# A graph layer whose rows are fetched one by one: three groups more of lead, and one place more in the ring

## The chip, the cores and the metric

The kernel runs on one core of a Trainium2 chip. Its time is the device time of one execution in microseconds. Beside it stands a profile: one further execution, recorded by the hardware profiler.

The engines are named as the profile names them: PE is TensorE (PEld its weight loads), DVE is VectorE, ACT is ScalarE, POOL is GpSimd and SP is SyncE. SP, ACT and POOL also issue DMAs, each from a queue of its own, and each engine works through its own instructions in order.

## The reference

x has 12500 rows (nodes) of 256 numbers. There are 200000 edges; edge e leads from node src[e] to node dst[e], and the edges are sorted by dst. All is float32.

```python
h = jnp.maximum(_layernorm(x, axis=-1), 0.0)
agg = jax.ops.segment_sum(h[src], dst, num_segments=N)
z = (1.0 + eps_gin) * h + agg
t = jnp.dot(z, W1) + b1                          # 256 -> 512
t = jax.nn.relu(_batchnorm(t, g1, bt1))          # over all 12500 rows
conv_out = jnp.dot(t, W2) + b2                   # 512 -> 256
out = x + jax.nn.relu(_batchnorm(conv_out + h, g2, bt2))
```

So for each edge a row of h is gathered, rows with the same destination are summed, and two dense layers follow, each with a normalisation that needs sums over all nodes.

## The kernel before, in words

**Groups.** The 200000 edges are cut into tiles of 128 edges and the tiles into 131 groups of 12 (GT); the last group has 3. Since the edges are sorted, the 1536 edges of a group lead to few neighbouring nodes. The loop over groups (L789 to L847, and a second one from L856 for the last five) is written out by hand: the order in which each engine gets its instructions is the order in the source.

**One group, i.** POOL gathers its rows, 128 at a time, with one indirect DMA for each tile (`gather`, L567). DVE builds a matrix of zeros and ones from the destinations (`edges`, L606). PE multiplies the two and adds up over the 12 tiles (`sums`, L625, the matmul on L639). The sums are copied (`hold`), brought to their place by a second matmul (`put`, L696) and added by DVE into a chunk zc of 512 nodes (`add`, L707). Chunks are loaded by SP from a table h_cols (`z_load`, L597) and scaled by ACT (`z_scale`). A chunk whose groups are all in is multiplied by W1 (`slice_of`, L719), its statistics are taken, and the product is stored by ACT in a table t_tab (`take`, L735).

**Lead-in.** The rows of h must be computed first. While that is done (NCH is 25 chunks of 512 rows), the first 30 groups (LEAD) gather rows of x and normalise them after the gather. From group 30 on POOL gathers rows of h from the table h_tab.

**Where gathered groups lie.** `gather(i + AHEAD)` is issued at step i, with AHEAD 3. In the lead-in the groups go round four places (L569): some are tiles of the pool `ring`, with RING buffers, the others the pairs `lands` (gta with 8 tiles, gtb with 4), which the first two groups used too. From group 33 on (L570) all groups go to `ring` alone. POOL may write into a place when PE has summed the group that lay there.

**Rows fetched one by one.** To take work from POOL, two queues each fetch one tile out of every nine groups: `hf` on SP (tile 0 of the group, called one_s) and `af` on ACT (tile 1, one_a). A `Fetcher` (L454) begins at step 28; at each step it issues the next lot of single-row DMAs (L500), 128 rows in nine steps (SP_PACE and ACT_PACE are (9, 1)), in lots of 16 (LOADS), after loading their addresses into registers (L494). Which groups it serves is settled on L463: `begin + SPARE + 9 * k`, for k = 1, 2, and so on. The set for such a group is asked for in the nine steps that end SPARE + 1 steps before it. Before PE uses a fetched tile it waits for a semaphore that counts the 128 rows (`use`, L508); within a group these tiles come last (L632). SP also issues the loads of zc, and ACT the stores of t_tab, in the same queues and in program order.

**After the loop** the second half of the kernel (from L905) loads t_tab, applies the first normalisation, multiplies by W2, and so on. Its tiles lie where the loop's tiles lay.

Of the kernel before, what the change touches and what calls it, by code (L numbers as in the profile page):

```python
# [22 lines left out]
LEAD = 30  # L23
EARLY = 2
FRONT = 3
RING = 2
LOW = 8
LOADS = 16
SP_PACE = (9, 1)
ACT_PACE = (9, 1)  # L30
SPARE = 4
XIN = 1


# [7 lines left out]
def kernel(  # L42
# [306 lines left out]
    def fast():  # L349
# [24 lines left out]
        with ExitStack() as fs:  # L374
# [14 lines left out]
            with ExitStack() as es:  # L389
                ln = es.enter_context(tc.tile_pool(name="ln", bufs=2))  # L390
                ring = es.enter_context(tc.tile_pool(name="ring", bufs=RING))
                sel = es.enter_context(tc.tile_pool(name="sel", bufs=2))
# [61 lines left out]
                class Fetcher:  # L454

                    def __init__(self, eng, kind, table, pace, begin, end, slots, tag):
# [5 lines left out]
                        while True:  # L462
                            g = begin + SPARE + -(-(len(self.groups) + 1) * self.over // self.per)  # L463
                            if g >= end:
# [102 lines left out]
                def gather(i):  # L567
                    t0, n = groups[i]
                    k = i % (AHEAD + 1)  # L569
                    if i >= LEAD + AHEAD or k > AHEAD - RING:  # L570
                        ga = ((0, GT, ring.tile([P, GT, D], F32, name="gt")),)
# [880 lines left out]
```

## Time and profile before

| what | value |
|---|---|
| median of 3 runs | 2481.28 us (2460.36 to 2487.5) |
| the profiled execution | 2484.16 us |
| its span, first to last instruction | 2482.4 us |
| mean granted TensorE clock | 0.766 of full speed |
| busy, PE / PEld / DVE / ACT / POOL | 62% / 40% / 34% / 17% / 62% |
| gathers from h_tab, POOL (L578) | 1171, 948 ns each in the middle |
| rows fetched one by one, SP and ACT (L500) | 1280 each |

"Idle before" a group of instructions is time in which its engine had nothing running, and the name behind the arrow is what ended that time: an engine and line, a DMA, "issue" (the engine waited for nothing that the profile shows) or "remote" (a semaphore whose sender the profile doesn't name). A name with a small q (SPq, ACTq) is the engine's queue, where DMAs are issued. In a timeline a line is: start, length, engine, source line, operation, tiles written and read, count, and in brackets the idle time before it. A line with a count over 1 merges several instructions. Matmuls in float32 have two records for each tile, so a group shows 24.

### The profile page before, as it was taken

What the parts mean: (1) busy time and instruction counts of PE and PEld (TensorE: products, weight loads), DVE (VectorE), ACT (ScalarE), POOL (GpSimd) and SP (SyncE); (2) the same over time, 40 slices, a digit from 0 to 9 for tenths busy, and PEclk for the clock granted to TensorE, in tenths of its full rate; (3) what the DMA queues carried; (4) which work ended last, traced back from release to release, by engine and by line L of the source; (5) the groups of instructions that cost most, each with busy time, mean ns of one, the idle gap of its engine ahead of it and who ended that gap; (6) DMA issues with size and microseconds to landing.
All of it is one profiled execution on the core that took longest, in us unless ns stands there. A gap on an engine that the chain in (4) does not pass through costs nothing.

```text
span 2482.4 us, 20597 instructions
## 1 busy us (share of the span) xinstructions
PE 1530.5 (62%) x4856; PEld 1003.3 (40%) x4856; DVE 852.0 (34%) x1344; ACT 424.8 (17%) x777; POOL 1540.6 (62%) x1589
## 2 busy tenths in 40 slices
PE   2564566555766665666655565656556666656997
PEld 1453444434434443434433344334333443434445
DVE  5454455432222222222222122122211222222897
ACT  4465455530000000000000000000000000001554
POOL 7566666565566666676666666665666666653550
PEclk9676777777777776777777777777777776777999
DMA  6566666443343333333433333343334333542988
GB/s 175 164 207 200 190 191 195 146 121 95 104 119 101 112 110 110 108 108 108 118 100 113 104 112 112 109 114 101 108 107 118 107 106 108 159 140 74 320 310 338
DMA packets 150290, 349.84 MB, mean 141 GB/s; under 512 B 32956, under 2 KB 63308, under 8 KB 150158
## 3 DMA queue, kind: packets, MB, share of 16 engines
q0 software_dynamic: 74048, 202.28, 29.2%
q1 hardware_dynamic: 45688, 105.80, 12.3%
q10 hardware_dynamic: 30422, 40.35, 4.7%
q8 instruction: 41, 0.67, 0.1%
q14 instruction: 91, 0.75, 0.1%
HBM read 284.29 MB, written 64.00 MB: 140 GB/s over the span
## 4 chain that ended last, share of the span: by engine, by line
issue 27%; POOL 20%; PE 16%; another core or an unknown queue 14%; SPq 11%; DVE 6%; ACT 4%; DMA 2%; PEld 0%; ACTq 0%; DVEq 0%; PEldq 0%; POOLq 0%
POOL gt L578 20%; SPq L500 10%; PE ps L639 6%; PE one L991 2%; PE ph L727 2%; DVE stg L422 2%; PE pq L991 1%; PE pr L991 1%; PE pz L702 1%; ACT gta L446 1%; DMA gt<-h_tab,srcT 1%; DVE oh L610 1%; SPq L494 1%; ACT ht L446 1%
## 5 line engine op out<-in xcount | busy, mean ns | idle before, releaser
L578 POOL DMA_INDIRECT gt<-h_tab,srcT x1171 | 1110.2, 948 | 601.7 <-issue 343.5
L639 PE MATMUL ps<-gt,oh 128*128 128x256 f32 x2648 | 841.3, 449 | 427.4 <-issue 286.7
L639 PEld LDWEIGHTS ps<-gt,oh 128*128 128x128 f32 x2648 | 559.2, 221 | 690.2 <-issue 373.4
L604 ACT ACTIVATE zc<-zc,gin 128x1024 f32<-128x1024 f32 (+1 forms) x25 | 28.1, 1125 | 1594.1 <-issue 979.3
L702 PE MATMUL pz<-at,zs 128*128 128x256 f32 x516 | 186.2, 474 | 156.3 <-issue 149.6
L689 DVE COPY zs<-ps 128x256 f32<-128x256 f32 x97 | 40.7, 420 | 649.0 <-remote 407.5
L738 DVE BATCH_NORM_STATS2 st<-ph 128x6 f32<-128x512 f32 x96 | 66.4, 693 | 495.8 <-remote 452.8
L727 PE MATMUL ph<-zc,w1s 128*128 128x512 f32 (+1 forms) x392 | 201.7, 640 | 40.9 <-DVE hc L561 25.9
L610 DVE TENSOR_TENSOR oh<-col,dstT 128x1536 f32<-128x1536 f32 x129 | 225.1, 1746 | 0.0
L578 POOL DMA_INDIRECT gt<-in_x_dram,srcT x168 | 159.3, 948 | 88.7 <-issue 57.1
L702 PEld LDWEIGHTS pz<-at,zs 128*128 128x128 f32 x516 | 123.1, 241 | 218.7 <-issue 200.0
L717 DVE TENSOR_TENSOR zc<-pz,zc 128x512 f32<-128x512 f32 (+7 forms) x185 | 91.7, 519 | 213.4 <-remote 127.4
L578 POOL DMA_INDIRECT gta<-in_x_dram,srcT x112 | 106.2, 948 | 50.6 <-issue 25.1
L727 PEld LDWEIGHTS ph<-zc,w1s 128*128 128x128 f32 x392 | 83.1, 214 | 107.0 <-issue 63.6
L549 PE MATMUL ph<-ident,ht 128*128 128x128 f32 x196 | 41.9, 346 | 108.1 <-issue 58.9
L639 PE MATMUL ps<-gta,oh 128*128 128x256 f32 x272 | 71.5, 398 | 39.9 <-issue 39.7
L446 ACT ACTIVATE gt<-gt,nbg,rsg 128x256 f32<-128x256 f32 x168 | 85.0, 588 | 11.9 <-issue 10.1
L549 PEld LDWEIGHTS ph<-ident,ht 128*128 128x128 f32 x196 | 29.3, 175 | 126.1 <-issue 77.3
L578 POOL DMA_INDIRECT gtb<-in_x_dram,srcT x56 | 53.1, 948 | 39.8 <-issue 11.6
L639 PE MATMUL ps<-gtb,oh 128*128 128x256 f32 x136 | 51.4, 524 | 42.7 <-issue 22.8
L639 PEld LDWEIGHTS ps<-gta,oh 128*128 128x128 f32 x272 | 54.3, 200 | 52.3 <-issue 45.5
L639 PE MATMUL ps<-one_s,oh 128*128 128x256 f32 x20 | 9.1, 546 | 104.0 <-DMA one_s<-h_tab 57.0
(195 smaller groups left out, 1308.7 us busy)
## 6 DMA issues: line engine op xcount, KB each, us to landing
t_tab<-ts ACTq DMA_DIRECT2D x96, 256.0 KB
one_s<-h_tab SPq DMA_DIRECT2D x1280, 1.0 KB
one_a<-h_tab ACTq DMA_DIRECT2D x1280, 1.0 KB
gt<-h_tab,srcT POOLq DMA_INDIRECT x1171
xt<-in_x_dram SPq DMA_DIRECT2D x24, 512.0 KB
h_tab<-ht ACTq DMA_DIRECT2D x24, 512.0 KB
h_cols<-hc SPq DMA_DIRECT2D x24, 512.0 KB
zc<-h_cols SPq DMA_DIRECT2D x24, 512.0 KB
```

Of the source, the lines that this page charges most:

```text
L422: nc.vector.bn_stats(st[:, c : c + 2, :].rearrange("p c s -> p (c s)"), two.rearrange("p c d -> p d c"),)
L446: nc.scalar.activation(slot(to, c), slot(v, c), AF.Relu, bias=nb[:, c : c + 1], scale=rs[:, c : c + 1])
L500: d = self.eng.dma_start(self.tiles[g][q % P : q % P + 1, q // P, :].bitcast(U8), self.bytes[bass.ds(v, 4 * D)].rearrange("(o e) -> o e", ...
L549: nc.tensor.transpose(ph[:, c * P : (c + 1) * P], ht[:, c, d * P : (d + 1) * P], ident)
L578: nc.gpsimd.indirect_dma_start(out=slot(ga, t - t0)[:rows], out_offset=None, in_=x if i < LEAD else h_tab, in_offset=bass.IndirectOffsetOn ...
L610: nc.vector.tensor_tensor(ohs[i][:, :n, :], col[:, :P].unsqueeze(1).to_broadcast([P, n, P]), dstT[:, t0 : t0 + n].unsqueeze(2).to_broadcas ...
L639: nc.tensor.matmul(ps, lhsT=oh[:rows, j, :], rhs=fetched[:rows], start=(j == order[0]), stop=(j == order[-1]))
L702: nc.tensor.matmul(pz[:, d, :n], lhsT=zs[:, d * P : (d + 1) * P], rhs=at[:, :n], start=True, stop=True)
L717: nc.vector.tensor_add(side, pz[:, :, a - lo : b - lo], side)
L727: nc.tensor.matmul(ph[:, :n], lhsT=w1s[:, d, f * P : (f + 1) * P], rhs=zc[c][:, d, :n], start=(d == 0), stop=(d == DC - 1),)
L738: nc.vector.bn_stats(st1[:, f, c, :], ph[:, :n])
L991: nc.tensor.matmul(ps, lhsT=w[:, k, :], rhs=t[:, k, :], start=(k == 0), stop=(k == DC - 1))
```

## The change

Two constants. SPARE sets how many groups ahead of its use a fetched set has to be complete (L463); with 7 in place of 4 the groups that use fetched tiles are 44, 53, ... 125 and no more 41, 50, ... 122. They are ten for each queue, as before. RING is the number of buffers of the pool that holds gathered groups; in the lead-in (L570) three of the four places are then tiles of the ring and one is a pair of `lands`, and from group 33 on three groups can lie gathered, not two. A buffer takes 12 KB of each partition.

```diff
 EARLY = 2
 FRONT = 3
-RING = 2
+RING = 3
 LOW = 8
 LOADS = 16
 SP_PACE = (9, 1)
 ACT_PACE = (9, 1)
-SPARE = 4
+SPARE = 7
 XIN = 1
```

## The prediction

> **What bounds the kernel now.** I read the views in this order: the page, the stretches by stage, POOL's own order of time, the waits of the fetched rows, and SP's queue. The profiled execution took 2484.16 us, of which the span is 2482.4; the runs shown have a median of 2481.28, so the sum below starts at 2484.2 and stands 3 us above that median. A measurement of this kernel can tell about 1% (25 us) from no change: its three runs lie 27 us apart.
>
> The page's head, and the stretches, each with its length and the busy time of PE, PEld, DVE, ACT, POOL:
>
> ```profile
> span 2482.4 us, 20597 instructions
> ...
> 40.00:532.50 492.50, 274.58 (x1002) 205.27 (x1003) 241.80 (x446) 263.21 (x551) 313.53 (x332) 0.73 0.57 177
> 532.50:892.50 360.00, 227.05 (x704) 149.70 (x704) 94.46 (x143) 20.89 (x38) 230.18 (x243) 0.76 0.37 107
> 892.50:1199.60 307.10, 190.38 (x562) 121.27 (x561) 72.67 (x108) 3.44 (x3) 202.38 (x215) 0.73 0.38 110
> 1199.60:2118.80 919.20, 550.01 (x1673) 358.66 (x1672) 216.46 (x322) 11.48 (x10) 599.35 (x633) 0.74 0.38 109
> 2118.80:2284.00 165.20, 97.88 (x316) 65.52 (x316) 32.97 (x58) 8.84 (x16) 89.63 (x95) 0.76 0.44 132
> 2284.00:2482.40 198.40, 183.04 (x572) 96.98 (x572) 170.58 (x222) 106.83 (x142) 75.95 (x34) 0.97 0.84 305
> ```
>
> The first is the lead-in, the last the second half of the kernel, which the change leaves as it is. Between them, POOL is the pace: 215 gathers in 307.1 us are 1.428 us each, 633 in 919.2 us are 1.452. What one takes without a wait, and what comes on top, is in POOL's timeline (start, length, idle before and its releaser):
>
> ```profile
> 987.50 0.95 POOL L578 DMA_INDIRECT gt<-h_tab,srcT  x1 [4.67 <-remote]
> ...
> 1016.35 0.95 POOL L578 DMA_INDIRECT gt<-h_tab,srcT  x1 [0.30 <-issue]
> 1022.01 0.95 POOL L578 DMA_INDIRECT gt<-h_tab,srcT  x1 [4.71 <-remote]
> 1023.26 0.95 POOL L578 DMA_INDIRECT gt<-h_tab,srcT  x1 [0.31 <-issue]
> ...
> 1053.75 0.95 POOL L578 DMA_INDIRECT gt<-h_tab,srcT  x1 [4.49 <-remote]
> ```
>
> A gather is followed by the next 1.25 us later. Every 34.5 us (987.50 to 1022.01: two groups, 24 gathers) POOL stops for 4.5 to 4.7 us. That looks like a ring with too few places; what PE and DVE do just before the stop says more:
>
> ```profile
> 999.62 1.88 PE L727 MATMUL ph<-zc,w1s 128*128 128x512 f32 x4
> ...
> 1010.18 0.59 PE L639 MATMUL ps<-gt,oh 128*128 128x256 f32 x1 [2.21 <-issue]
> 1012.98 0.59 PE L639 MATMUL ps<-gt,oh 128*128 128x256 f32 x1 [2.22 <-issue]
> ...
> 1021.60 0.70 DVE L738 BATCH_NORM_STATS2 st<-ph 128x6 f32<-128x512 f32 x1 [17.23 <-remote]
> ...
> 1023.24 6.67 PE L639 MATMUL ps<-gt,oh 128*128 128x256 f32 x24
> 1029.75 1.03 PE L702 MATMUL pz<-at,zs 128*128 128x256 f32 x4
> ```
>
> While POOL gathers, PE falls to one matmul in 2.8 us, with "issue" as the reason, that is for nothing the profile shows. About 4 us after POOL has stopped it is fast again (24 matmuls in 6.67 us), and only then do DVE and POOL see what PE had finished long before: DVE's statistics at 1021.60 had waited 17.23 us for a slice that PE had done at 1001.5. SP is in the same state: its register move takes 29 ns in the middle and up to 1420.
>
> ```profile
> L500 SPq MOVE one_s<-h_tab x1280: 1/29/1420, 499.7 to 2149.6; - x183
> L500 SPq DMA_DIRECT2D one_s<-h_tab x1280: 2/228/1422, 500.1 to 2151.0; - x183
> ```
>
> So the stop is not only a wait for a place; it is also when PE, SP and ACT get their work through. Two groups per stop is the pace, and a third place does not change what PE gets done per stop. I give this reading more weight than any other, though its cause cannot be seen.
>
> **The change part by part.** *SPARE 4 to 7.* The ten fetched sets of rows per queue stay ten; the groups that use them move from 41, 50, ... 122 to 44, 53, ... 125. SP and ACT issue the same instructions in the same order, no DMA more or less; POOL leaves out the same 20 gathers, three groups later. What it aims at are PE's waits for one_s:
>
> ```profile
> 754.35 0.59 PE L639 MATMUL ps<-one_s,oh 128*128 128x256 f32 x2
> ...
> 1060.23 0.59 PE L639 MATMUL ps<-one_s,oh 128*128 128x256 f32 x2
> ...
> 1533.36 1.22 PE L639 MATMUL ps<-one_s,oh 128*128 128x256 f32 x2 [20.81 <-PEq L510]
> 1693.19 1.22 PE L639 MATMUL ps<-one_s,oh 128*128 128x256 f32 x2 [27.92 <-DMA one_s<-h_tab]
> 1845.79 1.22 PE L639 MATMUL ps<-one_s,oh 128*128 128x256 f32 x2 [16.82 <-DMA one_s<-h_tab]
> 2002.79 1.22 PE L639 MATMUL ps<-one_s,oh 128*128 128x256 f32 x2 [26.18 <-PEq L510]
> 2150.42 1.22 PE L639 MATMUL ps<-one_s,oh 128*128 128x256 f32 x2 [12.23 <-DMA one_s<-h_tab]
> ```
>
> Five waits, 104 us of PE. But PE is not the pace. Four of them lie in the stretch to 2118.8, and there a gather took 1.452 us against 1.428 in the stretch without waits: 0.024 x 633 = 15 us is the most that the four can have cost. Per group the two stretches give 17.06 us (307.1 / 18, groups 50 to 68) and 17.02 (919.2 / 54, to group 122): by that count they cost nothing. The bounds are 0 and 15, and up to 12 more for the fifth.
>
> How many waits go? SP issued 1280 rows from 500.1 to 2151.0: 1.29 us each, 165 us for a set, against 153.5 us for nine groups at 17.06. It loses 11.5 us per set, and over nine sets 104. The first set was there at about 500 + 165 = 665, 89 us before its use at 754; three groups more make that 140, which lasts for all ten. But SP owes part of its rate to the waits, in which POOL stops too. Here is a stretch without any:
>
> ```profile
> 1171.61 42.27 SPq L500 DMA_DIRECT2D one_s<-h_tab  x27
> ```
>
> That is 1.57 us a row, 201 for a set; at this rate SP falls 47 us behind per set and is late again from the fourth or fifth on. So I expect two or three short waits to stay, late in the loop, and take 8 us of the 0 to 27 as gained.
>
> *RING 2 to 3.* Behind the lead-in POOL then needs the sums of a group one earlier. In the steady part I cost this at nothing, by the reading above. Its effect is at the two ends. Where the rotation of four places ends, and in the last groups, POOL waits for PE by name:
>
> ```profile
> 629.97 0.95 POOL L578 DMA_INDIRECT gt<-h_tab,srcT  x1 [12.74 <-PE ps L639]
> ...
> 2167.14 0.95 POOL L578 DMA_INDIRECT gt<-h_tab,srcT  x1 [4.92 <-remote]
> 2228.89 0.95 POOL L578 DMA_INDIRECT gt<-h_tab,srcT  x1 [16.97 <-PE ps L639]
> ```
>
> The first should shrink to an ordinary stop of 4.7 (8 us gained), the second should go (17 gained), since the place that it waits for is then that of the group before. Against it, PE has one group more to sum when POOL is done: undisturbed 6.67 us, with the placing (1.03) and a slice (1.88) 9.6.  Net about 16; the bounds are 0 (PE's late groups set the end anyway) and 25.
>
> In the lead-in four places rotate as before, but only one of them, not two, is the split pair of tiles gta and gtb, which can be refilled piece by piece. POOL's waits at gta, of what the two pairs show the larger part, are
>
> ```profile
> POOL gta L578 <- remote: 16.1, 8, 4.6
> ```
>
> 2 us each; seven groups with a whole tile instead lose between 0 and 16 us, and I take 4.
>
> The tiles of the second half keep their addresses, and the third place lies under yT tiles. SP loads those when the last sum (the first line) is over, so nothing is later there:
>
> ```profile
> L681 PE MATMUL pz<-oh,gt x12: 272/275/340, 2282.3 to 2283.7; 128*128 128x84 f32 x8, 64*128 64x84 f32 x4
> ...
> 2295.49 2.49 SPq L974 DMA_DIRECT2D yT<-h_cols  x4
> ```
>
> The sum: 2484.2 - 8 - 16 + 4 = 2464.
>
> **The rivals.** *Slower, by long bursts.* The point that decides is whether PE's news of the group before the last reaches POOL before it has done 24 gathers. If it does, POOL goes on to 36 while PE stands at one matmul in 2.8 us, and the stop after it is longer. The trace has one burst of 36, from 2167.1 to 2211.9, with the stop of 16.97 behind it:
>
> ```profile
> 2167.10:2228.90 61.80, 34.13 (x37) 0.78 0.49 153
> ```
>
> 61.8 us for 36 gathers are 1.717 each. For all 1171 gathers of the loop that would be 1171 x (1.717 - 1.44) = 324 us, 2808 (1.44 is 34.5 / 24); with a stop of 8 us, 36 x 1.253 + 8 = 53.1, 1.475 each, 41 us, 2525. I take the near end, since nothing but the loop's end shows the long stop. Against it: in the steady part what PE finished 14 us after a stop (the slice at 1001.5, POOL having started again at 987.5) wasn't seen before the next, and with three places PE, a group further behind, finishes the deciding group after 1.7 groups of 9.6 us, at about 16.
>
> *Nothing moves.* SP stays the bound for the late groups, so rows asked for 7 groups ahead are no more complete 7 ahead than now 4; and if the row waits go, the loads of zc, which stand in SP's queue behind the rows, are late in their place. They nearly are now:
>
> ```profile
> 1824.05 0.36 SPq L600 DMA_DIRECT2D zc<-h_cols  x1
> ...
> 1827.86 1.15 ACT L604 ACTIVATE zc<-zc,gin 128x1024 f32<-128x1024 f32 x1 [103.71 <-DMA zc<-h_cols]
> ...
> 1829.04 0.29 DVE L717 TENSOR_TENSOR zc<-pz,zc 128x128 f32<-128x128 f32 x1 [4.55 <-issue]
> ```
>
> DVE adds into that chunk 5 us after its load was issued. PE may run about two and a half groups further before the adds hold it, no three. Then only the ends gain, and the lead-in's loss eats that: 2480.
>
> *The ring is simply short.* Then a third place removes the stops: 1171 x (1.43 - 1.255) = 205 us, 2279. SP's rows forbid the whole of it, since at 1.57 us each they need 2010 us from 500 on; half is 2380. The trace speaks against it with PE's 2.8 us, which a place does not cure. The Trainium skill has a rule for this rival ("Perfetto Trace Analysis", Optimization Strategy): gaps that repeat alike on the engine that should be saturated can mean too few buffers for the next tile. By it the repeated 4.7 us is a lack of places; the trace agrees that the gaps repeat, not that places alone are what is lacking.
>
> **How the numbers follow.** Forecast 0.50 (2440 to 2482, centred at 2464), nothing moves 0.20 (2472 to 2500), long bursts 0.21 (2510 and up), ring simply short 0.09 (below 2440). Faster by over 1% (below 2459) takes 0.27 from the forecast's lower half and the last rival's 0.09: 0.36. Slower by over 1% (above 2509) is the long bursts, 0.21. The rest, 0.43, lies within 1%. The range leaves out most of the short ring and the worse half of the long bursts: 2425 to 2520.
>
> **What would show it.** Right: POOL still in bursts of 24 with stops of 4.5 to 5 us; 17 us per group in the middle; at most three one_s waits over 10 us; the waits at about 630 and 2229 gone or short; the second half starting at about 2265 and not 2284. The prediction is wrong if bursts of 36 appear, if the stops vanish, or if the rows' waits turn out to set POOL's pace after all, so that a loop without them loses the 27 us and more.

## The result, and the profile after

| | kernel before | changed kernel |
|---|---|---|
| median | 2469.84 us (14 runs, 2454.57 to 2487.5) | 2457.69 us (14 runs, 2447.74 to 2469.38) |
| ratio | 1 | 0.9948, 95% interval 0.9927 to 0.997 |
| the profiled execution | 2484.16 us | 2451.47 us |
| its span | 2482.4 us | 2449.7 us |

The change gains 12 us, half a per cent. The two profiled executions lie 32.7 us apart, because that of before is near the slow end of its runs and that of after near the fast end of its own. So terms read from the two traces add up to 32.7 us, of which some 20 are scatter.

One thing has to be said ahead of the experiments, as their numbers can't be understood without it. They ran on seven chips. On two of them the kernel before takes 2464 and 2472 us, and in the kernels profiled there POOL stops after 24 gathers most of the time, as in the profile of the prediction. On the other five it takes 2136 to 2141 us, and the traces from there have no such stops. I call them chips with stops and chips without. Each run was compared with the kernel before on its own chip.

First the stretches of the changed kernel (length; busy time of PE, PEld, DVE, ACT, POOL with their instructions; clock, DMA share, GB/s), the first three with the bounds used for before, the next two with the ends of their own work:

```profile
40.00:532.50 492.50, 285.40 (x1034) 213.17 (x1035) 253.17 (x465) 271.84 (x571) 318.20 (x337) 0.75 0.58 180
532.50:892.50 360.00, 210.34 (x664) 147.68 (x664) 86.48 (x128) 11.34 (x18) 234.59 (x249) 0.72 0.38 108
892.50:1199.60 307.10, 175.62 (x572) 124.83 (x570) 72.57 (x108) 3.45 (x3) 203.26 (x216) 0.73 0.38 110
1199.60:2119.70 920.10, 531.70 (x1670) 372.81 (x1670) 216.42 (x322) 11.47 (x10) 602.75 (x638) 0.72 0.38 110
2119.70:2250.80 131.10, 85.55 (x317) 62.00 (x315) 33.53 (x58) 8.82 (x16) 73.17 (x79) 0.80 0.49 147
2250.80:2449.70 198.90, 183.14 (x575) 97.08 (x573) 172.35 (x223) 106.75 (x142) 74.03 (x33) 0.97 0.85 304
```

In the middle little has moved: 216 gathers in 307.1 us (215 before), 638 in 920.1 (633 in 919.2). The lead-in and the stretch behind it have 5 and 6 gathers more than before. The last stretch of the loop is 131.1 us and was 165.2. The second half is 198.9 us and was 198.4.

POOL's timeline says the same (start, length, and in brackets the idle time before and its releaser):

```profile
613.20 0.94 POOL L578 DMA_INDIRECT gt<-h_tab,srcT  x1 [4.63 <-remote]
...
988.19 0.94 POOL L578 DMA_INDIRECT gt<-h_tab,srcT  x1 [4.80 <-remote]
...
1022.66 0.95 POOL L578 DMA_INDIRECT gt<-h_tab,srcT  x1 [4.76 <-remote]
...
1057.30 0.94 POOL L578 DMA_INDIRECT gt<-h_tab,srcT  x1 [4.95 <-remote]
...
2192.15 0.94 POOL L578 DMA_INDIRECT gt<-h_tab,srcT  x1 [4.29 <-remote]
2210.27 0.94 POOL L578 DMA_INDIRECT gt<-h_tab,srcT  x1 [3.44 <-PE ps L639]
```

The rhythm is that of before, 34.5 us for 24 gathers, 4.8 of them a stop. The wait of 12.74 us at 629.97 stood before the first gather of group 35; that gather now starts at 613.20, after a wait of 4.63. The wait of 16.97 at 2228.89 stood before group 128, which now starts at 2192.15 after 4.29; one more stop of 3.44 follows. The waits for fetched rows have gone altogether. Here is the group of matmuls on one_s, with the idle time of PE before it, and SP's two groups of issues:

```profile
L639 PE MATMUL ps<-one_s,oh x20: 379/379/586, 799.2 to 2171.7; 128*128 128x256 f32 x20
...
  issue: 4.4, 4
```

```profile
L500 SPq MOVE one_s<-h_tab x1280: 2/29/1407, 493.8 to 2147.0; - x183
L500 SPq DMA_DIRECT2D one_s<-h_tab x1280: 3/228/1413, 495.1 to 2147.7; - x183
```

SP is done with its rows at 2147.7, and was at 2151.0: asking further ahead doesn't make it issue faster.

Counting POOL's rows by group gives the 33 us by place. The first number is the time from the first gather of the stretch to the first one behind it; a stop is here what the starts of two gathers in it lie apart beyond 1.252 us:

| groups | before: us, stops | after: us, stops | gained, us |
|---|---|---|---|
| 0 to 32 (lead-in) | 583.4, 87.6 | 575.7, 79.9 | 7.7 |
| 33 to 40 | 144.9, 24.7 | 138.7, 18.5 | 6.2 |
| 41 to 85 | 765.7, 102.1 | 763.4, 99.9 | 2.3 |
| 86 to 122 (row waits before) | 635.2, 91.9 | 627.9, 82.0 | 7.3 |
| 123 to 130 | 129.9, 21.3 | 119.8, 13.7 | 10.1 |

SPARE has moved the last fetched pair of tiles from group 122 to group 125. So POOL has two gathers more in the fourth row and two fewer in the last, 2.5 us each way: by their stops alone these two rows gained 9.9 and 7.6 us.

### The profile page after: what moved, and what is told of

It reads as the page before. It is cut to its first block, busy times and chain, and to the rows that moved or that the text cites. A ratio compares the mean times of both kernels' runs of the same rounds, so it can differ in the third digit from the quotient of the medians.

```text
span 2449.7 us, 20490 instructions
## 1 busy us (share of the span) xinstructions
PE 1479.2 (60%) x4856; PEld 1023.5 (42%) x4856; DVE 855.1 (35%) x1344; ACT 423.5 (17%) x777; POOL 1535.6 (63%) x1589
## 3 DMA queue, kind: packets, MB, share of 16 engines
q0 software_dynamic: 74048, 202.28, 29.6%
## 4 chain that ended last, share of the span: by engine, by line
issue 38%; SPq 36%; PE 11%; another core or an unknown queue 5%; ACT 4%; DVE 3%; DMA 1%; ACTq 0%; POOL 0%; DVEq 0%
SPq L500 33%; SPq L494 3%; PE ps L639 2%; ACT gt L446 2%; PE one L991 2%; PE pr L991 1%; PE pq L991 1%; DVE stg L422 1%; PE ph L727 1%; PE ph L549 1%; SPq L600 1%; ACT ht L446 1%; PE pz L702 1%; PE pq L1020 1%
## 5 line engine op out<-in xcount | busy, mean ns | idle before, releaser
L578 POOL DMA_INDIRECT gt<-h_tab,srcT x1171 | 1106.9, 945 | 582.1 <-issue 342.3
L639 PEld LDWEIGHTS ps<-gt,oh 128*128 128x128 f32 x2816 | 617.5, 220 | 716.4 <-issue 617.1
L578 POOL DMA_INDIRECT gt<-in_x_dram,srcT x252 | 238.2, 945 | 120.4 <-issue 87.1
L717 DVE TENSOR_TENSOR zc<-pz,zc 128x512 f32<-128x512 f32 (+7 forms) x185 | 91.8, 519 | 257.9 <-ACT zc L604 89.9
L446 ACT ACTIVATE gt<-gt,nbg,rsg 128x256 f32<-128x256 f32 x252 | 126.4, 588 | 5.7 <-DVE rsg L438 3.4
L422 DVE BATCH_NORM_STATS2 stg<-gt 128x6 f32<-128x512 f32 x126 | 79.4, 689 | 18.4 <-DMA gt<-in_x_dram,srcT 14.1
L578 POOL DMA_INDIRECT gta<-in_x_dram,srcT x56 | 53.0, 946 | 36.6 <-issue 18.4
L639 PE MATMUL ps<-gta,oh 128*128 128x256 f32 x160 | 48.4, 431 | 28.9 <-issue 28.5
L694 DVE TENSOR_SCALAR at<-col,shift 128x256 f32<-128x256 f32 x129 | 61.2, 475 | 5.0 <-remote 5.0
L1012 POOL TENSOR_TENSOR ax<-ax,by 128x1024 f32<-128x1024 f32 x10 | 24.9, 2487 | 46.6 <-ACT by L969 39.9
L639 PEld LDWEIGHTS ps<-gta,oh 128*128 128x128 f32 x160 | 34.3, 217 | 43.7 <-issue 36.9
```

Source lines behind the costliest of these rows:

```text
L422: nc.vector.bn_stats(st[:, c : c + 2, :].rearrange("p c s -> p (c s)"), two.rearrange("p c d -> p d c"),)
L446: nc.scalar.activation(slot(to, c), slot(v, c), AF.Relu, bias=nb[:, c : c + 1], scale=rs[:, c : c + 1])
L578: nc.gpsimd.indirect_dma_start(out=slot(ga, t - t0)[:rows], out_offset=None, in_=x if i < LEAD else h_tab, in_offset=bass.IndirectOffsetOn ...
L639: nc.tensor.matmul(ps, lhsT=oh[:rows, j, :], rhs=fetched[:rows], start=(j == order[0]), stop=(j == order[-1]))
L717: nc.vector.tensor_add(side, pz[:, :, a - lo : b - lo], side)
```

## The experiments

The theory at the start was that of the prediction: PE gets two groups' work through at each stop of POOL, that is the pace, and the change gains at the two ends of the loop. Rivals: the row waits set the pace; the ring is simply short.

**One edit alone, and a fourth place.** Four kernels on one chip:

```diff
 # the first edit alone
-RING = 3
+RING = 2
 # the second edit alone
-SPARE = 7
+SPARE = 4
 # four places (RING 3, SPARE 7)
-                    if i >= LEAD + AHEAD or k > AHEAD - RING:
+                    if i >= NG - 6 or k > AHEAD - RING:
 # four places, with two split pairs in the lead-in
-                    if i >= LEAD + AHEAD or k > AHEAD - RING:
+                    if i >= NG - 6 or k > (1 if i < LEAD + AHEAD else 0):
```

> SPARE 7 with RING 2: the first of the two edits alone. Theory (PE's work gets through only while POOL stops; two groups per stop is the pace whatever waits stand in between): the waits for one_s go as in the changed kernel, and the time falls by no more than the 8 us of the prediction's step, 0.997 to 1.000 of the kernel before; bursts of 24 with stops of 4.5 to 5 us; the two named waits of 12.7 us (at 630) and 17.0 us (at 2229) stay within 2 us of that. Rival (the row waits set the pace): this edit alone gives the whole gain, 0.995 or less, and fewer than 17.0 us per group in the middle.

> RING 3 with SPARE 4: the second edit alone. Theory: it carries most of the gain, through the two ends of the loop (16 us by the prediction, less 4 in the lead-in): 0.994 to 0.997 of the kernel before; the waits for one_s stay, 12 to 28 us each, for nothing is asked earlier; the middle stays at 17.0 to 17.2 us per group. Rival (the row waits set the pace): 0.999 to 1.001, since the waits stay.

> The changed kernel with a fourth place: the pair of tiles that serves every fourth group in the lead-in goes on serving every fourth group up to group 124. Theory (PE's work per stop is the pace): still bursts of 24 gathers with stops of 4.5 to 5 us in the middle, 17.0 to 17.2 us per group, the time within 8 us of the changed kernel's. Rival one (the ring is short): the stops become rarer or shorter, 16.4 us per group or less, 60 us faster than the changed kernel. Rival two (long bursts): bursts of 36 and longer stops, 25 us or more slower.

> As the kernel with four places, but in the lead-in the four places are as in the kernel before (two tiles of the ring, two split pairs). Theory: the lead-in loses 4 us (0 to 16) in the changed kernel by its whole tiles, so this one is 0 to 16 us faster than the one with four places, 4 by the prediction's step. Rival: POOL is not the pace of the lead-in, and the two are alike within 3 us.

Measured, as ratios to the kernel before on that chip (2136.6 us): 0.9999 (0.999 to 1.0008), 1.0004 (0.9995 to 1.0013), 1.0001 (0.9992 to 1.001) and 1.0005 (0.9996 to 1.0014). Nothing moved anything, for this was a chip without stops. POOL's rows in the kernel with SPARE 7 and RING 2, first in its timeline and then, on the page, as a group:

```profile
984.73 0.95 POOL L578 DMA_INDIRECT gt<-h_tab,srcT  x1 [0.30 <-issue]
985.98 0.95 POOL L578 DMA_INDIRECT gt<-h_tab,srcT  x1 [0.30 <-PE ps L639]
987.23 0.95 POOL L578 DMA_INDIRECT gt<-h_tab,srcT  x1 [0.30 <-issue]
```

```profile
L578 POOL DMA_INDIRECT gt<-h_tab,srcT x1171 | 1106.9, 945 | 356.8 <-issue 333.7
```

The gather that depends on PE's sums (the second row) starts as early as any other. All 1543 gathers follow one another at 1.25 us without one stop, the idle time of POOL before the 1171 is 356.8 us (about 1171 x 0.30) and not 582.1 as in the changed kernel of the result, and with only two places. SP, in the same kernel:

```profile
L500 SPq MOVE one_s<-h_tab x1280: 29/29/38, 426.7 to 1653.0; - x183
L500 SPq DMA_DIRECT2D one_s<-h_tab x1280: 227/228/315, 426.8 to 1653.1; - x183
```

A register move takes 38 ns at most, not 1407, and in the kernel with SPARE 4 and RING 3 each one_s set is there 142 us or more before its use. So two places and four groups ahead are enough where PE, SP and ACT are not held up. The rival of the short ring, as the prediction put it, has fallen: in the result a third place left the stops, and here the ring of two places has none.

**The changed kernel itself, and more rows fetched,** on a second chip without stops:

```diff
 # more rows fetched (RING 3)
-SP_PACE = (9, 1)
-ACT_PACE = (9, 1)
-SPARE = 7
+SP_PACE = (4, 1)
+ACT_PACE = (4, 1)
+SPARE = 4
```

> The changed kernel itself, both edits together. Theory (the change pays only where PE and SP are held up while POOL gathers): where POOL gathers without stops, as in the five runs before this, the two edits together give 0.999 to 1.001; where the stops of 4.5 to 5 us are there, 0.993 to 0.997 again. Rival (the two edits act only together, by the ring giving time and the rows being asked for earlier): 0.995 or less also where there are no stops.

> RING 3 and SPARE 4, with a set of fetched rows for every fourth group of each queue, not every ninth (a pace of (4, 1)): 24 sets on SP and 23 on ACT for 10 and 10, so 27 gathers fewer on POOL. Theory: where POOL gathers without stops, POOL alone sets the end and SP's register moves take 29 ns, so the time falls by 27 x 1.25 = 34 us (0.984 of the kernel before); where SP is held up (1.29 us a row), a set takes 165 us and is asked for every 4 groups, 68 us, so PE waits for nearly every set and the kernel is 300 us slower or more. Rival (the rows' queues, or their 2 x 3000 single-row transfers, limit the loop even where nothing is held up): one_s waits of 10 us and more appear, and the time falls by less than 15 us or rises.

The changed kernel: 1.0003 (0.9994 to 1.0013). In these runs its gain exists only where there are stops. More rows: 2124.13 us, 0.9942 (0.9926 to 0.9959). No one_s wait appears, but only 12 of the 34 us come. What POOL's idle time before its gathers ended with, in that kernel:

```profile
  issue: 410.6, 1329
  DMA gt<-h_tab,srcT: 31.8, 65
```

POOL now waits a little for gathers that haven't landed: 1156 gathers of table rows from 453.5 to 1917.3 us are 1.266 each and not 1.250. That is 19 us in all, which leaves 15 of the 34. Both the theory (34) and the rival (one_s waits) missed that.

**Half the bytes,** on a third chip without stops. From group 34 on this kernel leaves out half of each gathered row; two more edits, not shown, let the sums read the gathered half twice:

```diff
-                            out=slot(ga, t - t0)[:rows], out_offset=None, in_=x if i < LEAD else h_tab,
+                            out=slot(ga, t - t0)[:rows, : D if i < LEAD + 4 else D // 2], out_offset=None,
+                            in_=x if i < LEAD else h_tab,
```

> The changed kernel, from group 34 on with gathers of half a row each (128 of the 256 columns; the sums use these columns twice, and the last two groups their first 128), so the output is another one; instructions, their order and their waits are the same. It asks whether PE's and SP's slow stretches, and the 1.25 us from one gather to the next, come from the bytes moved or from the issuing of the gathers. Theory one (the issuing): the next gather still follows after 1.25 us, and where stops stand between bursts they stay at 4.5 to 5 us, each 24 gathers; the time is within 1% of the changed kernel's on the same chip. Theory two (the bytes): the gathers follow each other in 0.8 us or less where POOL doesn't stop, or, where it does, PE's one matmul in 2.8 us is gone and with it the stops: 100 us or more faster.

2135.31 us, 0.999 (0.9978 to 1.0001). The gathers' queue moved 127.93 MB for 202.28, and a gather took what it took:

```profile
L578 POOL DMA_INDIRECT gt<-h_tab,srcT x1171: 903/944/958, 453.6 to 1929.5; - x196
```

So the 1.25 us doesn't go by the bytes; it is the same for 128 half rows as for 128 whole ones. Whether bytes play a part in the stops isn't told, since this chip had none.

**Half the sums** fell on a chip with stops, and it decides about the theory. From group 33 on this kernel leaves out 5 of the 12 tiles of a group's sum:

```diff
                     for k, j in enumerate(order):
                         if k in at:
                             at[k]()
+                        if i >= LEAD + AHEAD and k % 2 and j not in own and j not in (order[0], order[-1]):
+                            continue
```

> The changed kernel, from group 33 on with the sums of a group over half of its gathered tiles (7 matmuls for 12, the fetched ones all kept), so the output is another one; the gathers, their order and the row fetches are the same. Theory (where POOL stops, it is because PE is held up and gets two groups' work through per stop): with stops, fewer matmuls let POOL go on for 36 gathers and more at a time, 60 us or more faster than the changed kernel on the same chip; without stops POOL's 1.25 us per gather sets the pace and PE's work is hidden, so the time is within 4 us of the changed kernel's. Rival one (the ring is short, whatever PE does): with stops, they still come after each 24 gathers, time as the changed kernel's. Rival two (PE's sums are on the path where POOL doesn't stop): 20 us or more faster there.

2489.25 us for 2463.93, 1.0092 (1.0044 to 1.0139): slower than the kernel before, where the theory expected 60 us less than the changed kernel. POOL's timeline in the stretch with the smaller sums, with a row of PE:

```profile
1083.11 0.95 POOL L578 DMA_INDIRECT gt<-h_tab,srcT  x1 [4.20 <-remote]
...
1134.37 0.94 POOL L578 DMA_INDIRECT gt<-h_tab,srcT  x1 [6.46 <-remote]
...
1168.72 0.95 POOL L578 DMA_INDIRECT gt<-h_tab,srcT  x1 [4.58 <-remote]
...
1176.33 2.32 PE L641 MATMUL ps<-gt,oh 128*128 128x256 f32 x10
...
1203.08 0.95 POOL L578 DMA_INDIRECT gt<-h_tab,srcT  x1 [4.61 <-remote]
```

and the stretch to 2119.7:

```profile
1199.60:2119.70 920.10, 374.20 (x1114) 246.80 (x1114) 210.11 (x313) 11.47 (x10) 591.22 (x624) 0.66 0.38 107
```

PE has 1114 matmul records where it had 1670, and POOL mostly stops after 24 gathers for some 4.5 us, as ever (three times after 36, for 6.4 to 6.5). The stop before 1203.08 is the plainest. PE's last matmul ahead of it ended at 1178.65, 20 us before POOL stopped, and its next began at 1224.62; POOL stopped and went on while PE did nothing. So this stop is not for work that PE had still to do, and the amount of that work is not the pace. The theory's second half has fallen; rival one (the ring, whatever PE does) expected exactly these bursts, but it can't say why the same ring has no stops on the other chips. What fits both is that the news of a finished sum, once POOL has gathered for a while, doesn't get through until it stops. Why POOL stops after 24 gathers, and not after 12 or 36, isn't shown.

Why slower? The rows point to another wait. Five stops last 8.2 to 20.3 us and end with PE's sum, some 45 us more than as many ordinary stops, and the same chain stands in all five. Here is the one in the stop of 12.70 us that ended at 1230.53:

```profile
1195.73 0.69 SPq L600 DMA_DIRECT2D zc<-h_cols  x1
...
1222.93 1.15 ACT L604 ACTIVATE zc<-zc,gin 128x1024 f32<-128x1024 f32 x1 [120.11 <-issue]
...
1224.11 0.36 DVE L719 TENSOR_TENSOR zc<-pz,zc 128x192 f32<-128x192 f32 x1 [47.80 <-ACT zc L604]
1224.62 2.05 PE L704 MATMUL pz<-at,zs 128*128 128x256 f32 x4 [45.97 <-DVE zc L719]
```

The load of a chunk zc comes late out of SP's queue, ACT scales the chunk 27 us after, DVE has waited 47.80 us to add into it and PE 45.97. In this kernel DVE's adds waited 202.0 us for ACT's scaling; in the changed kernel it is 89.9, in the kernel before 27.8. That is the wait which the second rival of the prediction named. That it grows because PE gets further ahead fits the three figures, but no run shows it by itself.

The four traces with stops (before, after, this one and that of the next experiment) also give the length of a stop by the gathers ahead of it: after 12 gathers 2.77 us (the middle one of 66), after 24 gathers 4.71 (of 94), after 36 gathers 6.47 (of 4, one of which is the 16.97). Each gather adds about 0.155 us, (6.47 - 2.77) / 24, and each stop 0.9. By this estimate a gather costs 1.25 + 0.155 = 1.41 us there however the stops are cut, and longer bursts save only the 0.9. What takes the 1.41 us isn't shown.

**Four places and more rows fetched** fell on the other chip with stops.

```diff
-SP_PACE = (9, 1)
-ACT_PACE = (9, 1)
-SPARE = 7
+SP_PACE = (4, 1)
+ACT_PACE = (4, 1)
+SPARE = 4
-                    if i >= LEAD + AHEAD or k > AHEAD - RING:
+                    if i >= NG - 6 or k > AHEAD - RING:
```

> The kernel with four places up to group 124, SPARE 4, and a set of fetched rows for every fourth group of each queue, 27 gathers fewer on POOL. With three places this pace gained 12 of the 34 us that 27 x 1.25 makes, and POOL then waited in 68 places for the landing of earlier gathers or for PE, 32 us of its idle time put down to landings. Theory (with fewer gathers POOL catches up with the landings and with PE, and the place is what it lacks): four places give back 10 us and more, 0.985 to 0.990 of the kernel before where nothing is held up. Rival (what it lacks is not a place; the landings themselves set the end): 0.993 to 0.996 as with three places. Where POOL is stopped every 24 gathers and a row costs SP 1.3 us, 100 us slower than the kernel before or more, by rows that are not there in time.

3115.47 us for 2472.36, 1.2588 (1.2513 to 1.2662). PE's idle time before the matmuls on one_s, and on one_a:

```profile
L639 PE MATMUL ps<-one_s,oh x48: 379/634/796, 691.6 to 2885.1; 128*128 128x256 f32 x48
...
  PEq L510: 618.7, 37
```

```profile
L639 PE MATMUL ps<-one_a,oh x46: 379/634/796, 691.2 to 2775.3; 128*128 128x256 f32 x46
...
  PEq L510: 1058.2, 30
```

Here the rows set the pace, and POOL's stops are up to 51 us long. SP issued about 1900 of its 3072 rows during POOL's stops; in the changed kernel it was about 230 of 1280. The pace of fetching that gained 0.6% on a chip without stops, with a fourth place added, costs a quarter on one with them. Whether the place or the landings took the missing 22 us of the run with three places isn't told.

**The two halves again.** The first two kernels ran three times more, to part the two edits on a chip with stops.

> RING 3 with SPARE 4 once more, for a chip on which the stops of 4.5 to 5 us are there. Theory one (the ring's place saves time at the two ends of the loop): 0.993 to 0.997 of the kernel before on the same chip; the long burst of 36 gathers and the stop of 17 us near the end are gone, and the waits for one_s of 12 to 28 us stay. Theory two (SP is done with its last row at about 2150 us whatever is changed, and SPARE 7 puts that row three groups nearer to the end): RING alone gives 0.998 to 1.002, and the last gather stays near 2262 us. Where POOL gathers without stops, both expect 0.999 to 1.001 again, and the run tells nothing apart.

> SPARE 7 with RING 2 once more, for a chip on which the stops are there. Theory one (the third place carries the gain at the two ends): 0.998 to 1.001 of the kernel before on the same chip, the one_s waits gone and the long burst of 36 gathers with its stop of 17 us still there. Theory two (SP's last row comes at about 2150 us whatever is changed, and SPARE 7 puts it three groups nearer to the end): 0.993 to 0.997, the last gather at about 2230 us and no longer 2262. Where POOL gathers without stops, both expect 0.999 to 1.001 again, and the run tells nothing apart.

> RING 3 with SPARE 4 a third time, for a chip on which the stops are there; expected as in the run before of this kernel: by theory one (the third place saves time at the two ends) 0.993 to 0.997 of the kernel before, by theory two (SP's last row comes at about 2150 us, and SPARE 7 puts it three groups nearer to the end) 0.998 to 1.002. Without the stops 0.999 to 1.001 by both.

1.0002 (0.9993 to 1.0011), 1.0002 (0.9993 to 1.0011) and 1.0001 (0.9992 to 1.001), all on chips without stops. So which of the two edits carries the 12 us was not measured. For one stop the rows of the kernel before give an argument:

```profile
2183.64 0.70 PE L639 MATMUL ps<-gt,oh 128*128 128x256 f32 x2 [0.45 <-DMA gt<-h_tab,srcT]
2222.55 6.06 PE L639 MATMUL ps<-gt,oh 128*128 128x256 f32 x24
```

The first ends the sum of group 125, at 2184.3, the second is that of group 126, to 2228.6. With two places POOL's gather of group 128 needs group 126, and it started at 2228.89. With three it needs group 125, which was done 27 us before the burst ended at 2211.9; an ordinary stop after 36 gathers, 6.47 us, would have been left of the 16.97. That puts some 10 us to RING, argued and not shown. The rival is that SPARE gained them, by taking away PE's wait of 12.23 us at 2150.42. Against it, PE had made up for that wait by 2184: in the first row it waits 0.45 us for rows that have only just been gathered.

## Why the prediction came out right, point by point

**The pace of the middle: right, with a wrong reason.** Bursts of 24, stops of 4.8 us, 17 us a group: PE's sums of groups 50 to 122 start 17.02 us apart on average (894 to 2119.7 us), and 17.03 before. But the step "Two groups per stop is the pace, and a third place does not change what PE gets done per stop" ties the stop to PE's work, and the run with half the sums shows that it isn't: 556 matmul records fewer, mostly the same stops, and one of them while PE did nothing.

**SPARE: the sum about right, the waits wrong.** The step that failed is "So I expect two or three short waits to stay, late in the loop". None stayed. It took 1.57 us a row from a stretch within POOL's bursts as SP's rate for the whole loop; SP's rate with the stops stayed at (2147.7 - 495.1) / 1280 = 1.29 us. The estimate two sentences earlier, 140 us of lead less 104 lost, was the better one: the sets were issued to the last row 148.6 us ahead of their use at first, 13.6 at the seventh, and 23.1 at the last. (The first set of the kernel before was complete at 641 and not at 665, so its lead was 114 us and not 89; SP's rate isn't even.) The price, 8 us of 0 to 27, stands beside 9.9 us less of stops in groups 86 to 122; a part of that is scatter.

**RING at the two ends: about right in the traces, not shown to be RING's.** 16 us was the term, and by their stops groups 33 to 40 and 123 to 130 gained 6.2 + 7.6 = 13.8 in the two traces. The named waits of 12.74 and 16.97 us became 4.63 and 4.29: the first shrank to an ordinary stop, as forecast, and where the second was to go an ordinary stop stayed. No run with stops has one edit alone.

**The lead-in: wrong in sign.** The step "seven groups with a whole tile instead lose between 0 and 16 us, and I take 4" has 7.7 us gained in its place. The chips with stops gave three more readings of one stretch: groups 5 to 29 took 444.5 us before, and 438.1, 436.2 and 435.9 in three kernels with the changed lead-in. With one trace of before it can't be said how much of this is scatter. On a chip without stops the two lead-ins gave the same time.

**The sum.** The terms made -20 us from the profiled 2484.2. The traces differ by 32.7, the medians by 12. That the forecast, 2464, lies 6 us from the measured 2457.69 is in part luck: its start stood 14 us above the median of all runs of before, and its gain was 8 us too large. The second half began at 2250.8 and not at about 2265.

**The rivals.** Bursts of 36 didn't appear in the changed kernel. They did in the run with half the sums, and cost less than the rival said: from 1083.11 to 1134.37 are 51.3 us for 36 gathers, 1.42 us each, not 1.475. "Nothing moves" had a wait right, though not its price: the adds wait longer for zc (89.9 us for 27.8), and the time moved all the same. The short ring fell, with it the reading of repeated gaps as missing places that the prediction took from the Trainium skill ("Perfetto Trace Analysis", Optimization Strategy): the gaps repeat alike, and a place more leaves them at 4.8 us.

## What to carry to other kernels

When a stop repeats at a fixed rhythm, take work away from the engine that seems to need it before adding a buffer: if the stop stays, it isn't for that work. A buffer more then has little to give but where a rotation begins or ends, and a wait that lies beside a slower pace is worth little. A tuning that rests on an engine's rate, as the fetched rows do on SP's, can gain half a per cent on one chip and, with little changed, cost a quarter on another, so its slack is worth keeping.

## What the runs showed of the hardware that I had not expected

The same kernel takes 2136 to 2141 us on five chips and 2464 to 2472 on two. The whole difference lies where POOL issues indirect gathers: the second half, from the last sum to the end, takes 201.1 us on a chip without stops (1932.8 to 2133.9 in the kernel with half the bytes) and 198.9 in the changed kernel of the result. On the chips with stops, while POOL gathers, a register move on SP takes up to 1.4 us, PE gets to one matmul in 2.8 us, and a sum finished 20 us before POOL stopped was acted on only 4.6 us after. On the others none of this is to be seen. The granted TensorE clock doesn't explain it: in the middle it is 0.72 in the changed kernel of the result and 0.85 in the kernel with SPARE 7 and RING 2, but in the second half it is 0.97 in both, and with half the sums it fell to 0.66 while the usual stop stayed at 4.6 us. What sets such a chip apart, and whether it is the chip or a state that it was in, no trace here shows: each of the two was met once.
